# Loading the places of node ranges into VectorE registers: one by one next to their use, in place of ten per group

## The chip, the cores and the metric

The kernel runs on one NeuronCore of a Trainium2 chip. The metric is the device time of one execution in microseconds (us). Before the change it is 1736.52 us, the median of three runs that lie between 1736.14 and 1736.97.

The core has five engines that run side by side, each with its own stream of instructions: TensorE (PE, with its weight loads PEld), VectorE (DVE), ScalarE (ACT), GpSimd (POOL) and SyncE (SP), which here issues transfers. An engine carries out its stream in order. Waits for another engine, address arithmetic in registers and loads into registers stand in that same stream, beside the work on data. In the profile, a `q` behind an engine's name (DVEq) marks what the stream does itself; such instructions are not counted as busy.

## The reference

One layer of a graph network over 12500 nodes with 128 features and 400000 edges, sorted by the node they end at:

```python
Xs = X[src]
m_data = Xs @ W_data.T + b_data
m_ctrl = Xs @ W_control.T + b_control
msg = jnp.where((edge_types == 0)[:, None], m_data, m_ctrl)
agg = jax.ops.segment_sum(msg, dst, num_segments=X.shape[0])
out = agg + (X @ W_self.T + b_self)
x = _layernorm(x + jax.nn.relu(out), axis=-1)
```

The kernel first sums the raw features of the edges by end node and by type, and multiplies the sums by the weights afterwards; this gives the same, since the products are linear.

## The kernel before

The edges are cut into chunks of 128, and 125 chunks form a group; there are 25 groups (`NG`). A group's edges end at some 500 consecutive nodes, for which an accumulator `acc` (128 features by 2 types by 640 nodes) and a count `cnt` are kept in SBUF. Within a group the chunks form windows of two kinds, five of each (`NWIN` is 10):

- `p` windows (five chunks each): GpSimd gathers the 128 feature rows of a chunk from memory (`msg`, L828). The functions are `gathered` and its `chunk`.
- `e` windows (twenty chunks each, five in every fourth group, else four; 107 in all): the rows are picked out of the features held in SBUF by matrix products (L929, `got`), which ScalarE copies to `emsg` (L943). The function is `picked`. For each such window VectorE builds the matrices that sort the edges: `O`, `prod`, `ahead`, `found`, `rank`, `rm`, `rv`, `pick`, for every second window also `om_all`.

In both kinds VectorE builds matrices of zeros and ones from the end nodes (`psel`, `esel`, L533), TensorE multiplies them with the rows into `sums` in PSUM (L755), and VectorE adds the finished `sums` to `acc` and `cnt` (L817). Where in the 640 nodes a window is added depends on the data: that is its place, a whole number. All 250 places (25 groups of 10) are computed on the chip near the start, held to 0 through `R - WMAX` by a max and a min, and stored as `place_i`, one row of 250 numbers on one partition. An add whose address depends on a place needs the place in a register of VectorE; ahead of the add stands a register instruction that works out the address (`ISA` at L817 in the order of instructions, FUSED_REGOPS in the profile).

A `p` window adds to `cnt` and `acc` at one place, an `e` window to `acc` at another. There are 125 `p` windows and 107 `e` windows, so 232 places are used. When the last window of a group has been added, `pass_on` hands the nodes shared with the next group to that group's `acc` and `cnt` (L791, L792).

The order in which each engine gets its instructions is not the program's: a scheduler sorts them by what depends on what and by its own estimate of when things are ready. `tc.issue_after(ins)` asks only that an instruction stand behind `ins` in its engine's stream. Loads of places are queued behind the last add but one that was written ahead of them (`added[-2]`). The main loop runs over the 107 `e` windows and merges into each the chunks of `p` windows, the next windows' matrices, and a group's end (`finish`, L1036 to L1081).

Of the kernel before, what the change touches and what calls it, by code (L numbers as in the profile page):

```python
# [39 lines left out]
WMAX = max(AW, EW)  # L40
CHUNKS = PB + EC
M0 = 50
R = 640
# [17 lines left out]
def kernel(  # L61
# [53 lines left out]
    with ExitStack() as sx:  # L115
        short_path(sx, tc, const, ident, eps, wT, brow, bad, x, src, dst, etype,
                   (w_data, w_ctrl, w_self), (b_data, b_ctrl, b_self), out)
# [89 lines left out]
def short_path(ctx, tc, const, ident, eps, wT, brow, bad, x, src, dst, etype, ws, bs, out):  # L207
    nc = tc.nc
# [32 lines left out]
    raw = {}  # L241
# [500 lines left out]
        return [(0.6, lambda: half(0, NCELL))]  # L742


    acc, added, parts_in, at_places = {}, [], {}, {}

    def sums():
        return ps2.tile([P, 512], FP, name="sums")
# [53 lines left out]
    def place_of(g, i):  # L802

        parts_in[g] = parts_in.get(g, 0) + 1
        if g not in at_places:
            with tc.issue_after(added[-2].ins) if len(added) > 1 else ExitStack():
                _, at_places[g] = nc.values_load_multi_w_load_instructions(
                    raw["place"][0:1, g, :], engines=[nc.vector.engine], min_val=0, max_val=R - WMAX,
                    skip_runtime_bounds_check_because="places are held to this range by a max and a min on the chip",
                )  # L810
        return at_places[g][i]

    def accumulate(at, rows, ps, wide, width):

# [49 lines left out]
    def gathered(g, i):  # L864
# [3 lines left out]
        def add_counts():  # L868
            s["at"] = place_of(g, 2 * i)
            begin_acc(g)  # L870
            rows = cnt[g][:2 * CAP].rearrange("p (o r) -> p o r", o=1)
            accumulate(s["at"], rows, s["ps"][:2 * CAP, 2 * AW:], AW, AW)
# [36 lines left out]
    def picked(w, tiled, ending, before):  # L909
# [83 lines left out]
        def end():  # L993

            early, *more = tiled.get(turns, [lambda: None])
            early()
            gates = add(bounds[turns - 1], NQ)
            for u in more:
                u()
            accumulate(place_of(g, 2 * i + 1), acc_rows(g, 0, 2), s["ps"], EW, EW)  # L1000
            return gates
# [175 lines left out]
    for w in range(pairs):  # L1177
        g, i = each_e[w]
# [182 lines left out]
```

## Time and profile before

| | |
|---|---|
| median of three runs | 1736.52 us |
| the profiled execution | 1736.11 us, of which 1734.3 us is the span from its first to its last instruction |
| granted TensorE clock | 0.992 of full speed |
| PE busy | 1569.6 us, 91% of the span |
| DVE busy | 1550.3 us, 89% |
| POOL busy | 1292.2 us, 75% |
| ACT busy | 1246.5 us, 72% |
| loads of places (L807), in VectorE's stream | 25, from 1064 to 2315 ns each |

The busy share says how long an engine had work, not that it was the one everything waited for. For that the profile has the chain that ended last: it is followed back from the last instruction, at each step to what released that step. A group of instructions is shown with its line, engine, operation, what it writes and reads, its count, its total time and the mean of one, and behind the bar the engine's idle time just ahead of it with what ended that. In a timeline a bracket gives the same for one piece of work.

### The profile page before, as it was taken

What the parts mean: (1) busy time and instruction counts of PE and PEld (TensorE: products, weight loads), DVE (VectorE), ACT (ScalarE), POOL (GpSimd) and SP (SyncE); (2) the same over time, 40 slices, a digit from 0 to 9 for tenths busy, and PEclk for the clock granted to TensorE, in tenths of its full rate; (3) what the DMA queues carried; (4) which work ended last, traced back from release to release, by engine and by line L of the source; (5) the groups of instructions that cost most, each with busy time, mean ns of one, the idle gap of its engine ahead of it and who ended that gap; (6) DMA issues with size and microseconds to landing.
All of it is one profiled execution on the core that took longest, in us unless ns stands there. A gap on an engine that the chain in (4) does not pass through costs nothing.

```text
span 1734.3 us, 67322 instructions
## 1 busy us (share of the span) xinstructions
PE 1569.6 (91%) x28154; PEld 1229.6 (71%) x28154; DVE 1550.3 (89%) x3677; ACT 1246.5 (72%) x2251; POOL 1292.2 (75%) x1061
## 2 busy tenths in 40 slices
PE   0599998999899999999999999999999999999997
PEld 0376777777677777777777777777777777777776
DVE  7898999899798898998998998999998998998983
ACT  5777777677677676777776777776777776777675
POOL 0277888888878788778777787787788787778771
PEclk9999999999999999999999999999999999999999
DMA  7844454444454544454545454445444445444441
GB/s 202 293 130 128 126 154 123 141 151 130 124 157 126 157 136 141 138 157 130 156 131 150 139 150 134 147 117 170 143 148 137 144 137 154 138 145 132 125 126 57
DMA packets 148966, 248.22 MB, mean 143 GB/s; under 512 B 35937, under 2 KB 115260, under 8 KB 148652
## 3 DMA queue, kind: packets, MB, share of 16 engines
q1 hardware_dynamic: 85994, 134.45, 23.4%
q0 software_dynamic: 50032, 102.98, 22.3%
q10 hardware_dynamic: 12626, 6.40, 1.4%
q8 instruction: 222, 3.64, 0.9%
q14 instruction: 92, 0.75, 0.1%
HBM read 226.24 MB, written 17.50 MB: 141 GB/s over the span
## 4 chain that ended last, share of the span: by engine, by line
PE 41%; DVE 39%; ACT 8%; issue 6%; DMA 4%; DVEq 1%; POOL 0%; SPq 0%; ACTq 0%; POOLq 0%
PE sums L755 18%; PE got L929 13%; DVE esel L533 5%; DVE prod L639 4%; ACT emsg L943 4%; PE side L1048 4%; DVE prod L634 3%; DVE pick L741 3%; DVE rv L674 3%; DVE found L641 3%; DVE prod L612 2%; PE side L622 2%; PE side L686 2%; DVE O L533 2%; ACT h L1078 2%
## 5 line engine op out<-in xcount | busy, mean ns | idle before, releaser
L828 POOL DMA_INDIRECT msg<-rows,idx_g x985 | 1222.6, 1241 | 320.4 <-issue 147.2
L943 ACT CAST emsg<-got 128x768 bf16<-128x768 f32 (+1 forms) x1070 | 949.3, 930 | 320.3 <-PE got L929 300.1
L755 PE MATMUL sums<-esel,emsg 128*128 128x176 bf16 x7704 | 693.1, 240 | 3.9 <-DVE acc L817 3.4
L755 PEld LDWEIGHTS <-emsg 128*128 128x128 bf16 x7704 | 566.7, 98 | 117.0 <-issue 108.2
L929 PE MATMUL got<-x,pick 128*32 128x384 bf16 x10486 | 572.9, 330 | 27.7 <-DVE pick L741 13.3
L929 PEld LDWEIGHTS <-pick 128*32 128x32 bf16 x10486 | 242.5, 96 | 155.4 <-issue 24.9
L533 DVE TENSOR_TENSOR esel<-code_col,code 128x1760 bf16<-128x1760 bf16 x321 | 292.1, 910 | 14.5 <-PE sums L755 12.7
L755 PE MATMUL sums<-psel,msg 128*128 128x48 bf16 x2955 | 167.7, 184 | 14.7 <-DVE acc L817 13.0
L755 PEld LDWEIGHTS <-msg 128*128 128x128 bf16 x2955 | 138.8, 97 | 26.8 <-issue 23.7
L639 DVE TENSOR_TENSOR prod<-prod 128x1200 bf16<-128x1200 bf16 x214 | 133.7, 625 | 4.8
L634 DVE TENSOR_TENSOR prod<-O,ahead 128x2000 bf16<-128x2000 bf16 x107 | 128.4, 1200 | 2.5
L533 DVE TENSOR_TENSOR O<-cell_col,blk 128x2000 bf16<-128x2000 bf16 x107 | 127.4, 1191 | 0.9 <-ACT blk L437 0.7
L741 DVE TENSOR_SCALAR pick<-pick,lane_f 128x3200 bf16<-128x3200 bf16 x107 | 113.2, 1058 | 0.8 <-DMA pick<-there 0.8
L817 DVE TENSOR_TENSOR acc<-acc,sums 128x176 f32 (+2 forms) x232 | 66.2, 285 | 52.5 <-PE sums L755 42.2
L904 POOL DMA_INDIRECT both<-rows,idx x54 | 64.2, 1189 | 54.6 <-ACT emsg L943 28.5
L686 PE MATMUL side<-rv,O 128*128 128x64 bf16 x2140 | 83.3, 195 | 21.9 <-DVE rv L674 19.6
L533 DVE TENSOR_TENSOR psel<-near_col,near 128x1200 bf16<-128x1200 bf16 x125 | 95.8, 767 | 0.1
L686 PEld LDWEIGHTS <-O 128*128 128x128 bf16 x2140 | 79.0, 100 | 23.6 <-DVE rv L674 19.8
L674 DVE TENSOR_TENSOR rv<-rm,vals 128x1280 bf16<-128x1280 bf16 x107 | 87.7, 820 | 0.0
L641 DVE TENSOR_REDUCE found<-prod 128x20 f32<-128x600 bf16 x107 | 82.8, 774 | 2.6
L612 DVE TENSOR_TENSOR prod<-O 128x1000 bf16<-128x1000 bf16 x107 | 71.9, 672 | 0.0
L622 PEld LDWEIGHTS <-ltri 128*128 128x128 bf16 x1284 | 41.1, 96 | 38.1 <-issue 36.0
(192 smaller groups left out, 1566.8 us busy)
## 6 DMA issues: line engine op xcount, KB each, us to landing
pick<-there SPq DMA_DIRECT2D x106, 800.0 KB
msg<-rows,idx_g POOLq DMA_INDIRECT x985
acc<-acc_start SPq DMA_DIRECT2D x23, 640.0 KB
rows<-x SPq DMA_DIRECT2D x6, 1344.0 KB
xs<-in_x_dram SPq DMA_DIRECT2D x99, 62.5 KB
out_dram<-h SPq DMA_DIRECT2D x99, 62.5 KB
xt<-in_x_dram ACTq DMA_DIRECT2D x6, 896.0 KB
cnt<-cnt_start SPq DMA_DIRECT2D x22, 160.0 KB
```

Of the source, the lines that this page charges most:

```text
L533: nc.vector.tensor_tensor(sel.rearrange("p n (w t) -> p n w t", t=2), col[:rows].rearrange("p (o w t) -> p o w t", o=1, t=2).to_broadcast( ...
L612: nc.vector.tensor_add(h[:, :2 * CQ], s["O"][:, :2 * CQ], s["O"][:, 2 * CQ:])
L634: nc.vector.tensor_tensor(prod[:, :, :NCELL], s["O"], ahead.rearrange("p (o j) -> p o j", o=1).to_broadcast([P, EC, NCELL]), op=OP.mult,)
L639: nc.vector.tensor_add(prod[:, :, :h], prod[:, :, :h], prod[:, :, h:2 * h])
L641: nc.vector.tensor_reduce(found, prod[:, :, :h], AX.X, OP.add)
L674: placed[:] = [nc.vector.tensor_tensor(rv.rearrange("p c v (r t) -> p c v r t", t=2), rm.rearrange("p c (o r t) -> p c o r t", o=1, t=2).t ...
L686: nc.tensor.matmul(s["rk"][:m, :2 * CAP], s["held"][:, c * NCELL:c * NCELL + m], s["rv"][:, c].rearrange("p v r -> p (v r)"), start=(c == ...
L741: nc.vector.tensor_scalar(t, t, lane_f, None, op0=OP.is_equal)
L755: last = nc.tensor.matmul(out, msg[:, j * D:(j + 1) * D], sel, start=(start and j == 0), stop=stop, skip_group_check=True)
L828: return nc.gpsimd.indirect_dma_start(out=msg, out_offset=None, in_=rows3[:, :], in_offset=bass.IndirectOffsetOnAxis(ap=codes["p", g][0][: ...
L929: last = nc.tensor.matmul(ps[CAP * a:CAP * (a + 1), :], slots[w]["pick"][:, a * NQ + q, :], x3[:, 4 * q + a - a0].rearrange("p j d -> p (j ...
L943: s["out"] = nc.scalar.copy(msg[:, :n], ps[:, :n, :3 * D])
```

## The change

The ten places of a group were loaded by one call into ten registers, when the group's first place was needed, and without a range test. Now each place is loaded by a call of its own into a register, where its window is about to be added, and each load is followed by a test in registers that the value lies between 0 and `R - WMAX`.

```diff
-    acc, added, parts_in, at_places = {}, [], {}, {}
+    acc, added, parts_in = {}, [], {}
...
         parts_in[g] = parts_in.get(g, 0) + 1
-        if g not in at_places:
-            with tc.issue_after(added[-2].ins) if len(added) > 1 else ExitStack():
-                _, at_places[g] = nc.values_load_multi_w_load_instructions(
-                    raw["place"][0:1, g, :], engines=[nc.vector.engine], min_val=0, max_val=R - WMAX,
-                    skip_runtime_bounds_check_because="places are held to this range by a max and a min on the chip",
-                )
-        return at_places[g][i]
+        with tc.issue_after(added[-2].ins) if len(added) > 1 else ExitStack():
+            return nc.vector.value_load(raw["place"][0:1, g, i:i + 1], min_val=0, max_val=R - WMAX)
```

In VectorE's stream there were 25 instructions TENSOR_LOAD for places; there are now 232, and behind each stand two register instructions for its test. Nothing else is added or removed, but the scheduler puts other instructions into another order too. Lines behind the change move up by five: L817 is L812 in the changed kernel, L791 is L786.

The first place is VectorE's stream where group 1 begins, in the kernel before: `esel` and `O` are matrices for `e` windows, the adds to `acc` and `cnt` are those of L817, and L791 and L792 pass group 0's shared nodes on.

```order
L533 TENSOR_TENSOR esel<-code_col,code 128x1760
L533 TENSOR_TENSOR O<-cell_col_143,blk_1333 128x2000
L817 ISA
L817 TENSOR_TENSOR acc<-acc,sums 128x2x88
L807 TENSOR_LOAD place_i
L817 ISA
L817 TENSOR_TENSOR cnt<-cnt,sums 64x120
L817 ISA
L817 TENSOR_TENSOR acc<-acc,sums 128x2x40
L792 TENSOR_TENSOR cnt<-cnt 128x140
L791 TENSOR_TENSOR acc<-acc 128x2x140
```

The same place in VectorE's stream of the changed kernel:

```order
L533 TENSOR_TENSOR esel<-code_col,code 128x1760
L806 TENSOR_LOAD place_i
L806 ISA x2
L806 TENSOR_LOAD place_i
L806 ISA x2
L533 TENSOR_TENSOR O<-cell_col_143,blk_1330 128x2000
L812 ISA
L812 TENSOR_TENSOR acc<-acc,sums 128x2x88
L812 ISA
L812 TENSOR_TENSOR cnt<-cnt,sums 64x120
L812 ISA
L812 TENSOR_TENSOR acc<-acc,sums 128x2x40
```

The load of ten, which stood between two adds, is gone, and two single loads stand behind `esel`, ahead of `O`.

The second place is VectorE's stream a few windows into group 13, in the kernel before: `rs` and `nm` are two short steps of a group's end on 125 rows by 4 numbers, and `parts` and `pk` prepare the next group.

```order
L533 TENSOR_TENSOR esel<-code_col,code 128x1760
L1072 RECIPROCAL rs<-sd 125x4
L511 TENSOR_SCALAR parts<-idx_g 128x125
L1074 SCALAR_TENSOR_TENSOR nm<-mv,rs 125x4
L817 ISA
L817 TENSOR_TENSOR acc<-acc,sums 128x2x88
L512 TENSOR_SCALAR parts<-idx_g 128x125
```

And in the changed kernel:

```order
L533 TENSOR_TENSOR esel<-code_col,code 128x1760
L1067 RECIPROCAL rs<-sd 125x4
L1069 SCALAR_TENSOR_TENSOR nm<-mv,rs 125x4
L806 TENSOR_LOAD place_i
L806 ISA x2
L511 TENSOR_SCALAR parts<-idx_g 128x125
L512 TENSOR_SCALAR parts<-idx_g 128x125
L515 SCALAR_TENSOR_TENSOR pk<-idx_g,vals_23323 128x125
L533 TENSOR_TENSOR psel<-near_col,near_21310 128x1200
L812 ISA
L812 TENSOR_TENSOR acc<-acc,sums 128x2x88
L533 TENSOR_TENSOR esel<-code_col,code 128x1584
```

A single load with its test now stands behind two short instructions, of which the second needs the first, and the add to `acc` comes three instructions later than it did.

The third place is again VectorE's stream in group 0, one window ahead of the first place, where `om_all`, which waits for a small product of TensorE, and `psel` change places. Before:

```order
L817 TENSOR_TENSOR acc<-acc,sums 128x2x40
L533 TENSOR_TENSOR psel<-near_col,near_887 128x1200
L558 TENSOR_SCALAR om_all_193<-slot_col,side 128x7x64 x2
L533 TENSOR_TENSOR O<-cell_col_144,blk_1333 128x2000
L817 ISA
L817 TENSOR_TENSOR acc<-acc,sums 128x2x88
```

In the changed kernel:

```order
L812 TENSOR_TENSOR acc<-acc,sums 128x2x40
L558 TENSOR_SCALAR om_all_193<-slot_col,side 128x7x64 x2
L806 TENSOR_LOAD place_i
L806 ISA x2
L533 TENSOR_TENSOR psel<-near_col,near_887 128x1200
L533 TENSOR_TENSOR O<-cell_col_144,blk_1330 128x2000
L812 ISA
L812 TENSOR_TENSOR acc<-acc,sums 128x2x88
```

`om_all` moves ahead of `psel`, and the load stands right behind it.

## The prediction

> **What bounds the kernel now.** I read the page's head and its shares first, then the chain that ended last, then what VectorE's own stream did around the loads.
>
> ```profile
> span 1734.3 us, 67322 instructions
> PE 1569.6 (91%) x28154; PEld 1229.6 (71%) x28154; DVE 1550.3 (89%) x3677; ACT 1246.5 (72%) x2251; POOL 1292.2 (75%) x1061
> PE 41%; DVE 39%; ACT 8%; issue 6%; DMA 4%; DVEq 1%; POOL 0%; SPq 0%; ACTq 0%; POOLq 0%
> ```
>
> TensorE and VectorE are both busy for nine tenths of the span, and the chain runs through them in equal parts, 41% and 39%. So there is no single bound: the two hand work to each other with little slack. A pause of VectorE is paid where the chain is on VectorE, and is mostly swallowed where it is on TensorE.
>
> The loads of places are not busy time of VectorE, but they hold up its stream. These rows are from the view of one line's instructions (count, then least, median and largest duration), over the whole span and over two short windows:
>
> ```profile
> L807 DVEq TENSOR_LOAD <-place_i x25: 1064/1320/2315, 75.0 to 1660.8; - x25
> ...
> L807 DVEq TENSOR_LOAD <-place_i x1: 2315/2315/2315, 139.8 to 139.8; - x1
> ...
> L807 DVEq TENSOR_LOAD <-place_i x1: 1064/1064/1064, 488.8 to 488.8; - x1
> ```
>
> A load of ten comes in two sizes that alternate from group to group: 12 of the 25 take about 2.3 us, 12 about 1.07 us, and the first 1.32 us; together some 41.7 us. What such a load costs depends on what VectorE still has queued. In the timeline at the first of the two windows it has nothing, in that at the second it has a microsecond of work:
>
> ```profile
> 139.81 0.34 DVE L817 TENSOR_TENSOR acc<-acc,sums 128x176 f32 x1 [0.89 <-PE sums L755]
> ...
> 142.34 0.28 DVE L817 TENSOR_TENSOR cnt<-cnt,sums 64x120 f32 x1 [2.19 <-PE side L622]
> ...
> 142.81 1.31 PE L755 MATMUL sums<-esel,emsg 128*128 128x176 bf16 x15 [1.09 <-DVE acc L817]
> ...
> 489.27 1.05 DVE L741 TENSOR_SCALAR pick<-pick,lane_f 128x3200 bf16<-128x3200 bf16 x1
> 490.23 0.17 DVE L651 MAX8 top<-key 128x8 f32<-128x20 f32 x1
> 490.32 0.25 DVE L817 TENSOR_TENSOR cnt<-cnt,sums 64x120 f32 x1
> ```
>
> At 139.8 the stream had just been let go by TensorE, so the load began together with the add of 0.34 us, VectorE stood idle for 2.19 us, and TensorE then waited 1.09 us for `sums` to be freed. At 488.8 the load ran while VectorE worked off instructions that had been issued ahead; VectorE never stopped. So the stream runs ahead of the work, and only what a load takes beyond that lead is a pause.
>
> The chain in order of time shows what of these pauses was paid:
>
> ```profile
> 140.15 1.99 DVEq L807
> 142.14 0.08 issue
> 142.22 0.07 DVEq L817
> 142.29 0.05 issue
> ...
> 679.63 1.87 DVEq L807
> ...
> 814.85 0.36 DVEq L807
> ...
> 1337.94 0.36 DVEq L807
> ...
> 1599.92 2.17 DVEq L807
> ```
>
> The five pieces are 6.75 us; two more of 0.09 us are on the chain, so it holds 6.9 us of loads. That is what the change can take away for certain.
>
> **The change, part by part.** *Removed:* 25 loads of ten. By the chain the gain is 6.9 us. Its ends: nothing, if TensorE would have held up the same stretches, and 16 us, if none had been covered (41.7 us by VectorE's 39% of the chain). I take 6.9, since it is measured at these very loads.
>
> *Added:* 232 loads of one, each with a test. The trace has one load of a single number on VectorE and one test, both at the end of the kernel, where the flag for the fallback path is read:
>
> ```profile
> L119 SPq TENSOR_LOAD <-bad x1: 480/480/480, 1713.1 to 1713.1; - x1
> ...
> L119 SPq FUSED_REGOPS  x1: 187/187/187, 1713.6 to 1713.6; - x1
> L119 SPq SEQ_ASSERT  x1: 33/33/33, 1713.9 to 1713.9; - x1
> L119 PEldq TENSOR_LOAD <-bad x1: 713/713/713, 1724.0 to 1724.0; - x1
> L119 DVEq TENSOR_LOAD <-bad x1: 309/309/309, 1727.6 to 1727.6; - x1
> ...
> L817 DVEq FUSED_REGOPS  x357: 69/69/69, 76.4 to 1722.5; - x179
> ```
>
> The test is two instructions, 187 and 33 ns on SyncE. On VectorE the load is 0.31 us; the step from a load to the next register instruction is 0.08 us and from there on 0.05 us (the issue rows of the chain above). With the test's first half as on SyncE a place costs 0.31 + 0.08 + 0.19 + 0.05 + 0.03 + 0.05 = 0.71 us of the stream; with that half at the 69 ns that VectorE's address instructions take, 0.59. I take 0.65 us: 151 us of stream in all, against 41.7 before.
>
> What of it becomes a pause depends on what stands ahead. In the order of the changed kernel, 99 of the 232 loads stand right behind an instruction of 0.65 us or more, most often `esel`; those are covered. The other 133 stand behind short ones, 0.28 us in the mean. The mean durations of the commonest are in the groups by shape:
>
> ```profile
> L533 DVE TENSOR_TENSOR esel<-code_col,code 128x1584 bf16<-128x1584 bf16 x107 | 104.2, 974 | 0.0
> ...
> L558 DVE TENSOR_SCALAR om_all<-slot_col,side 128x448 bf16<-128x448 bf16 x107 | 43.0, 439 | 5.3 <-PE side L552 3.7 <-ACT blk L437 0.9 <-ACT emsg L943 0.2
> L630 DVE TENSOR_REDUCE ahead<-side 128x100 bf16<-128x200 f32 x107 | 38.6, 361 | 32.9 <-PE side L622 31.9 <-issue 0.5
> ...
> L647 DVE SCALAR_TENSOR_TENSOR key<-rank,pk 128x20 f32<-128x20 bf16 x107 | 18.5, 173 | 0.0
> ...
> L1074 DVE SCALAR_TENSOR_TENSOR nm<-mv,rs 125x4 f32<-125x4 f32 x24 | 3.8, 157 | 0.2
> ```
>
> If only that one instruction covers (the stream was held until it began, as at 139.8), the pauses are 133 x 0.65 - 36.7 = 50 us, 36.7 being what the short ones take. If the two instructions ahead cover, 48 places are left with 10.7 us. I take the middle, 30 us, since both cases stand in the rows above. Of pauses scattered over VectorE's stream the end pays VectorE's share of the chain: 30 x 0.39 = 11.8 us. The ends are 3.1 us (two instructions cover, 0.59 us a place: 8 us of pauses) and 22.5 us (one covers, 0.71: 58 us).
>
> Behind a load in the stream waits whatever comes next. For 26 of the loads that is the address and the add to `acc` or `cnt`, which frees `sums` for TensorE, and for 13 the pass of `cnt` to the next group; who waits is TensorE, as at 142.81. No transfer is added, and the queues of SyncE and GpSimd hold the same transfers as before. At the end of the kernel the last loads stand ahead of adds that wait for TensorE, and cost nothing unless TensorE is done first.
>
> The Trainium skill's page "DMA: Bandwidth & Descriptors", section "Latency and other measured facts", speaks against the change: it gives a tensor load a floor of about 600 ns and says that the compiler unrolls four times to spread it. The trace has 309 ns on VectorE and 480 on SyncE, both below that floor, so by this case's rows it doesn't hold. With 0.60 in place of 0.31 a place would cost 0.94 us, the pauses would be 34 to 92 us by the two covers, and the sum, as an estimate from that page, 1754 us.
>
> *Moved:* the scheduler, which counts with the loads, puts other work elsewhere. By summing durations along both orders, most instructions keep their place: of the 107 adds that free an `e` window's `sums` some 15 come later and 11 earlier by over 0.2 us, of the adds of `p` windows 12 later and 24 earlier; `om_all` is earlier in 48 of 107 cases. What TensorE waits on these for now:
>
> ```profile
> PE sums L755 <- DVE acc L817: 16.4, 21, 1.8
> PE side L562 <- DVE om_all L558: 14.1, 26, 1.0
> ...
> PE side L504 <- DVE code_r L494: 10.4, 15, 0.9
> ```
>
> These are 41 us, and about a fifth of the places move, so I bound this term by 8 us either way and take nothing, as it goes both ways. The five steps on `bias` near the start move ahead of long work they stood between, and two loads go there; that is at most 2 x 0.65 us, inside the bounds.
>
> *Sum:* -6.9 + 11.8 + 0 = +4.9 us. The profiled execution took 1736.11 us, 0.4 below the median of 1736.52; against the median the forecast is 1741.4 us.
>
> **The rivals.**
>
> *The small pauses are hidden and the large ones go (faster).* Place: the group starts, as at 139.8, 679.6 and 1599.9. If two instructions cover nearly everywhere, the sum is -6.9 + 3.1 = -3.8, so 1732.7; with the order in its favour down to 1725. For it speaks the row at 490.23, where a whole microsecond is hidden, and that at the first place shown above the loads now stand behind `esel`. Against it: 133 loads stand behind short work. It decides when the pauses come to less than 6.9 / 0.39 = 17.7 us, 0.076 us a place.
>
> *It cancels.* The same with pauses between 9 and 27 us: within 0.2% of before, about what a measurement of this kernel can tell from no change (3.5 us), so 1733 to 1740.
>
> *A single load in the stream is dearer than at the end.* TensorE's queue took 713 ns for one number. At that a place costs 1.05 us, the pauses are 46 to 113 us, in the middle 79 x 0.39 = 31 us, and the time is 1761. The loads of ten, at 107 or 230 ns a number, speak against it.
>
> *The change does nothing to VectorE's stream* is excluded by the order: 232 loads stand in it.
>
> **How the numbers follow.** I give the forecast's case, slower by 3.5 to 15 us, 0.40; the dear load or an unlucky order beyond that 0.11; that it cancels 0.19; faster 0.30. So slower 0.51, same 0.19, faster 0.30. The range takes in the full gain with small pauses (-16 + 3.1, 1723.6) and the largest pauses with no gain (+22.5, 1759), and a little of the order's 8 us above: 1723 to 1763. The slower case alone spans 1740 to 1752.
>
> **What the profile of the changed kernel would show.** Right: 232 rows of loads at about 0.31 us each in VectorE's stream, with two register instructions behind; idle of 0.2 to 0.5 us behind short work ahead of many of them; none of 2 us; VectorE's busy time unchanged within 5 us; on the chain, pieces of the loads that add up to more than 6.9 us. Wrong: loads of 0.2 us or less, or DVE's idle time down by more than 10 us with TensorE's too, would make it faster; loads of 0.6 us or more would make it much slower. If the loads' share of the chain is small and the time differs still, it was the order.

## The result and the profile after

The changed kernel takes 1719.82 us (median of six runs, 1711.99 to 1723.35); the kernel before took 1735.88 us beside it (six runs, 1734.46 to 1736.97). The ratio is 0.9904 with a 95% interval of 0.9883 to 0.9924: it is faster by 1%, 16 us. The forecast was 1741.4 us and slower.

The page of the changed kernel, its span, its busy times and its chain by engine:

```profile
span 1718.0 us, 68009 instructions
...
PE 1557.0 (91%) x28154; PEld 1228.9 (72%) x28154; DVE 1556.2 (91%) x3677; ACT 1245.1 (72%) x2251; POOL 1290.1 (75%) x1061
...
DVE 42%; PE 35%; issue 8%; DMA 5%; ACT 4%; DVEq 2%; POOL 1%; ACTq 0%; POOLq 0%; SPq 0%
```

VectorE's busy time rose by 5.9 us, from 1550.3. What fell is the rest of its span: 1734.3 - 1550.3 = 184.0 us before, 1718.0 - 1556.2 = 161.8 us after. So the 16 us come out of the time in which VectorE has no work, although 207 more loads stand in its stream. These are the loads and their tests (count, then least, median and largest ns):

```profile
L806 DVEq TENSOR_LOAD <-place_i x232: 296/304/2044, 44.2 to 1706.0; - x116
L806 DVEq FUSED_REGOPS  x232: 183/190/206, 45.3 to 1706.3; - x116
L806 DVEq SEQ_ASSERT  x232: 23/23/31, 45.5 to 1706.6; - x116
```

They cost the stream what was forecast. The share of VectorE's own queue in the chain went up, from 1% to 2%: the loads and tests hold 26.0 us of the chain in 204 pieces, against 6.9 us for the loads of ten. By themselves they speak for a slower kernel. What fell is shown by VectorE's waits (total us, times, longest us), first before and then after:

```profile
DVE acc L817 <- PE sums L755: 42.2, 35, 7.9
DVE ahead L630 <- PE side L622: 31.9, 50, 2.9
DVE esel L533 <- PE sums L755: 12.7, 15, 1.4
...
DVE cnt L817 <- PE sums L755: 8.3, 9, 2.1
```

```profile
DVE acc L812 <- PE sums L755: 33.2, 32, 6.7
DVE ahead L630 <- PE side L622: 23.3, 44, 1.7
...
DVE esel L533 <- PE sums L755: 9.1, 17, 2.3
...
DVE psel L533 <- issue: 6.3, 16, 0.6
...
DVE cnt L812 <- PE sums L755: 1.3, 4, 0.6
```

The first two waits for TensorE are 17.6 us shorter, and the four rows of before, 95.1 us, are 66.9 us now. New are 6.3 us ahead of `psel` in small pieces. At the place at 139.8 us, where the load of ten had stopped VectorE for 2.19 us, the timeline of the changed kernel has one add behind the other without idle time:

```profile
138.95 0.34 DVE L812 TENSOR_TENSOR acc<-acc,sums 128x176 f32 x1
139.21 0.27 DVE L812 TENSOR_TENSOR cnt<-cnt,sums 64x120 f32 x1
139.40 0.22 DVE L812 TENSOR_TENSOR acc<-acc,sums 128x80 f32 x1
139.55 0.22 DVE L792 TENSOR_TENSOR cnt<-cnt 128x140 bf16<-128x140 bf16 x1
```

TensorE's busy time fell too, from 1569.6 to 1557.0 us, with the same products; that this alone does not shorten the kernel is seen below, where TensorE's order alone brings that busy time to 1562.3 us and the kernel is no faster. The granted clock is not the reason: its mean is 0.994 over the six runs, and 0.993 to 0.994 over the runs of the kernel before beside the first twelve experiments.

Two things had changed at once, the loads and the order in which the scheduler put the rest. The experiments take them apart.

### The profile page after: what moved, and what is told of

Read it like the earlier page. It is cut to its first block, busy times and chain, and to the rows that moved or that the text cites. A ratio compares the mean times of both kernels' runs of the same rounds, so it can differ in the third digit from the quotient of the medians.

```text
span 1718.0 us, 68009 instructions
## 1 busy us (share of the span) xinstructions
PE 1557.0 (91%) x28154; PEld 1228.9 (72%) x28154; DVE 1556.2 (91%) x3677; ACT 1245.1 (72%) x2251; POOL 1290.1 (75%) x1061
## 4 chain that ended last, share of the span: by engine, by line
DVE 42%; PE 35%; issue 8%; DMA 5%; ACT 4%; DVEq 2%; POOL 1%; ACTq 0%; POOLq 0%; SPq 0%
PE sums L755 15%; PE got L924 11%; DVE esel L533 6%; DVE prod L639 4%; DVE prod L634 3%; DVE pick L741 3%; DVE rv L674 3%; PE side L1043 3%; DVE found L641 3%; DMA both<-rows,idx 3%; DVE prod L612 2%; DVE psel L533 2%; ACT emsg L938 2%; DVE O L533 2%; DMA msg<-rows,idx_g 2%
## 5 line engine op out<-in xcount | busy, mean ns | idle before, releaser
L533 DVE TENSOR_TENSOR esel<-code_col,code 128x1760 bf16<-128x1760 bf16 x321 | 292.6, 912 | 11.8 <-PE sums L755 9.1
L812 DVE TENSOR_TENSOR acc<-acc,sums 128x176 f32 (+2 forms) x232 | 66.6, 287 | 34.1 <-PE sums L755 33.2
(192 smaller groups left out, 1562.3 us busy)
```

The costliest lines, as they stand in the source:

```text
L533: nc.vector.tensor_tensor(sel.rearrange("p n (w t) -> p n w t", t=2), col[:rows].rearrange("p (o w t) -> p o w t", o=1, t=2).to_broadcast( ...
```

## The experiments

Several kernels below have an engine's order prescribed. The same function does it in all: each instruction is made to be issued behind the one ahead of it in a list, without a semaphore; loads and tests of places are left out of the lists. Between two loads or orders everything else stays as it was.

```diff
+def in_given_order(tc):
...
+    for engine, text in _ORDER.items():
...
+        for a, b in zip(order, order[1:]):
+            tc.add_manual_dep(
+                mine[b], mine[a].name,
+                mybir.DependencyInfo(mybir.DependencyClass.NoSync, mybir.DependencyReason.DATA), reason="given order",
+            )
```

### Loads of ten in the changed kernel's order, single loads in the order of before

The kernel before, with the lists of all five engines taken from the changed kernel:

```diff
+_ORDER = {
+    'EngineType.Pool':
...
+    'EngineType.PE':
...
+        in_given_order(tc)
```

> Loads of ten as before the change, but every other instruction on every engine in the changed kernel's order. If the gain of 16 us came from the other order, this takes about 1720 us plus what the loads of ten cost against single ones, so 1715 to 1728. If it came from the loads themselves (no stops of 2.3 us at the starts of odd groups), this takes about 1736, 1732 to 1740.

The reverse is the same edit to the changed kernel, with the lists taken from before:

```diff
+        in_given_order(tc)
```

> Single loads with their tests as after the change, but every other instruction on every engine in the order of the kernel before. If the order gave the gain, this takes 1736 to 1741 us (the prediction's sum without a change of order). If the loads gave it, about 1720, 1715 to 1725.

Loads of ten in the new order: 1721.13 us, ratio 0.9915 (0.9895 to 0.9935). Single loads in the old order: 1742.62 us, ratio 1.0043 (1.0027 to 1.0058), where before took 1734.41 us. The order is worth the whole gain and the single loads, in the old order, cost 8 us, a little more than either expectation had. From the page and the waits of single loads in the old order:

```profile
span 1740.4 us, 67993 instructions
...
DVE 42%; PE 40%; issue 7%; ACT 6%; DMA 3%; DVEq 2%; SPq 0%; POOL 0%; ACTq 0%; POOLq 0%
```

```profile
DVE ahead L663 <- PE side L655: 28.6, 47, 1.4
DVE esel L566 <- PE sums L788: 18.1, 20, 2.4
...
DVE psel L566 <- issue: 11.6, 14, 3.3
```

Here too VectorE stands ahead of `psel`, 11.6 us that the profile puts down to "issue"; in 8.7 of them a load stands directly ahead in the stream. `esel` waits longer than before (18.1 us for 12.7). The adds' wait for `sums` is 12.5 us shorter than with loads of ten in the same order (29.7 for 42.2): a part of the pauses takes the place of waits. The two effects don't add up in full. In the new order loads of ten and single loads take the same time within their intervals; in the old one they differ by 8 us. Why the cost of the single loads is not seen in the new order stays open.

### Loads of ten, with rows that start at other addresses

The loads of ten had come in two sizes that alternate by group. A row of ten numbers is 40 bytes, so every other row starts 8 bytes off a multiple of 16. Two kernels in the order of before space the rows by 48 bytes; in one they start at a multiple of 16:

```diff
-        place_i = raw["place"] = keep.tile([1, NG, NWIN], I32, name="place_i")
+        wide = keep.tile([1, NG, 12], I32, name="place_i")
+        place_i = raw["place"] = wide[:, :, 0:0+NWIN]
```

> The kernel before, with the row of ten places stored 48 bytes apart in place of 40, so that each row starts at a multiple of 16 bytes; the order stays the same. If the size of a load of ten goes by where its row starts, all 25 take about 1.07 us. Then the loads' theory says 12 x 1.23 = 15 us less stop on VectorE, so 1722 to 1730; the order's theory says at most the share of it that was on the chain, 1732 to 1736.

and in the other 8 bytes behind it:

```diff
-        place_i = raw["place"] = keep.tile([1, NG, NWIN], I32, name="place_i")
+        wide = keep.tile([1, NG, 12], I32, name="place_i")
+        place_i = raw["place"] = wide[:, :, 2:2+NWIN]
```

> The same with each row starting 8 bytes behind a multiple of 16. If the start decides, all 25 loads take about 2.3 us, 13 x 1.23 = 16 us more stop on VectorE than before. The loads' theory: 1745 to 1753. The order's theory: 1736 to 1741.

The loads in the first and in the second:

```profile
L808 DVEq TENSOR_LOAD <-place_i x25: 1061/1066/1319, 76.9 to 1655.9; - x25
```

```profile
L808 DVEq TENSOR_LOAD <-place_i x25: 2279/2285/2527, 76.3 to 1667.3; - x25
```

Where the row starts makes the size: 1.07 or 2.28 us for the same ten numbers. The times are 1730.65 us (0.997, 0.9957 to 0.9983) and 1742.62 us (1.0044, 1.0029 to 1.006). Each lies between its two expected ranges, so neither theory had the size right. Between the two kernels the loads differ by 25 x (2.285 - 1.066) = 30.5 us of the stream and the times by 12.0 us, which is 39%; the intervals of the two ratios leave room for about 31 to 53%. That this is VectorE's share of the chain in the profile before doesn't confirm the prediction's rule, which took that share of the pauses and not of the loads' whole time. VectorE's idle time directly behind loads is 6.8 us in the first kernel and 15.4 us in the second, but 15.4 us in the kernel before as well, which takes 8 us less than the second. Where the second pays these 8 us isn't shown.

### Single loads without the test

The changed kernel without the range tests of the 232 places:

```diff
-            return nc.vector.value_load(raw["place"][0:1, g, i:i + 1], min_val=0, max_val=R - WMAX)
+            return nc.values_load(
+                raw["place"][0:1, g, i:i + 1], engines=[nc.vector.engine], min_val=0, max_val=R - WMAX,
...
+            )
```

> The changed kernel without the tests behind its loads; all other instructions keep the changed kernel's order. A place then takes 0.3 us of VectorE's stream in place of 0.6. If the pauses behind loads are paid by VectorE's share of the chain, 5 to 9 us less than the changed kernel, so 1711 to 1715. If they are mostly swallowed, 1717 to 1720.

1716.54 us, ratio 0.9903 (0.9886 to 0.992), where before took 1732.95: the same ratio as with the tests. In the new order 232 times 0.2 us of the stream are worth nothing that can be measured; the two intervals leave room for some 5 us.

### TensorE's order: more and fewer changes of size

In the new order TensorE changes less often between products with 32 and with 128 weight columns (1326 times for 1388), so this was a candidate. One kernel takes the changed kernel's order with 248 such changes more, by splitting 124 runs of products; the other takes the order of before with 84 fewer, by joining 46. Both differ from the given order in TensorE's list alone:

```diff
+    'EngineType.PE':
...
+        in_given_order(tc)
```

> The changed kernel with one product of sums put ahead of the last four row-picking products at 124 places of TensorE's order, so that TensorE changes between products with 32 and with 128 weight columns 248 times more often (1574 times, 1326 in the changed kernel, 1388 before); hardly anything else moves. If these changes, about 0.1 us each in the trace, are paid, and are part of the 16 us: 12 to 25 us more than the changed kernel, so 1732 to 1745. If the order's gain is about waits alone: 1718 to 1726.

> The kernel before, loads of ten, but at 46 places of TensorE's order a few small products that stood inside a run of row picking stand behind it, so that TensorE changes between 32 and 128 weight columns 1304 times in place of 1388. If the changes are paid: 4 to 8 us less, 1726 to 1731. If what waits for the moved products matters more: 1734 to 1745.

With the splits it takes 1713.34 us, ratio 0.9891 (0.9876 to 0.9907): no slower than the changed kernel. With the joins it takes 1732.17 us, ratio 1.0002 (0.9991 to 1.0013). TensorE's busy time does move, from 1557.0 to 1580.9 us with 248 changes more and from 1569.6 to 1561.0 us with 84 fewer, about 0.1 us a change both times. The Trainium skill's page "TensorEngine Tiling (Array Packing)", section "Key Properties", says that changing the tiling mode drains TensorE. The rise of the busy time agrees with that; no time of these two runs speaks for a price that the end pays here.

### One engine's order at a time

Loads of ten, with the changed kernel's order prescribed to TensorE alone, all others left to the scheduler:

```diff
+_ORDER = {
+    'EngineType.PE':
...
+}
...
+        in_given_order(tc)
```

> The kernel before, loads of ten, with TensorE's instructions alone in the changed kernel's order; the scheduler orders the other engines by itself, and VectorE's order then stands between the two kernels' orders. If TensorE's order is what gave the gain: 1717 to 1726, with TensorE busy about 1557 us. If it was VectorE's order: 1731 to 1737.

And to VectorE alone:

```diff
+_ORDER = {
+    'EngineType.DVE':
...
+}
...
+        in_given_order(tc)
```

> Loads of ten, and VectorE's own instructions alone forced into the changed kernel's order; TensorE, ScalarE, GpSimd and the queues are left to the scheduler. If VectorE's order carries the gain: 1717 to 1724 us, VectorE's idle time near 155 us as in the changed kernel. If the orders of several engines must fit together: 1730 to 1738 us, idle near 175 us as with TensorE's order alone.

TensorE's order: 1736.99 us, ratio 1.0027 (1.0014 to 1.004). VectorE's order: 1711.94 us, ratio 0.9872 (0.9857 to 0.9887), below the changed kernel's own 0.9904 and below the expected range. From the page and the waits with TensorE's order, then the same with VectorE's:

```profile
span 1736.9 us, 67341 instructions
...
PE 1562.3 (90%) x28154; PEld 1231.9 (71%) x28154; DVE 1554.7 (90%) x3677; ACT 1245.0 (72%) x2251; POOL 1287.3 (74%) x1061
```

```profile
DVE acc L846 <- PE sums L784: 43.6, 47, 3.2
DVE ahead L659 <- PE side L651: 32.1, 55, 1.6
```

```profile
span 1711.8 us, 67316 instructions
...
PE 1568.0 (92%) x28154; PEld 1224.9 (72%) x28154; DVE 1550.0 (91%) x3677; ACT 1247.2 (73%) x2251; POOL 1278.5 (75%) x1061
```

```profile
DVE ahead L659 <- PE side L651: 28.5, 45, 1.4
DVE acc L846 <- PE sums L784: 23.8, 26, 3.4
```

With VectorE's order the wait of the adds for `sums` is nearly halved (42.2 to 23.8 us), VectorE's busy time is that of before (1550.0 us), and its span without work is 161.8 us for 184.0: that is nearly the whole of the 22.5 us between the spans. So the changed kernel's order of VectorE is enough for the gain, and that of TensorE is not. It is not VectorE's order by itself, since the scheduler ordered the other engines anew: TensorE's stream there differs from that of before in 138 stretches and from that of the changed kernel in 130. (With TensorE's order prescribed, VectorE's differs from that of before in 119.) VectorE's new order with all others left as before was not run.

A part of the 22 us goes with the clock. The four runs with VectorE's order all have a granted clock of 0.998, where the kernel before had 0.994 in the mean of its 15 runs. Those 15 runs are longer by about 1 us for each 0.001 of clock less, so the estimate from them is 4 us, which is most of the way by which this kernel lies below the changed one. Whether the order raised the clock isn't shown. It is still the best of all these kernels, and it has loads of ten.

Against before, the changed kernel's list for VectorE differs in 254 short stretches of 2 to 22 instructions, 1237 of 3677 instructions in all.

### Other orders from the same scheduler

Three kernels change only behind which earlier add a load is queued, and leave the order to the scheduler. Loads of ten, issued earlier:

```diff
-            with tc.issue_after(added[-2].ins) if len(added) > 1 else ExitStack():
+            with tc.issue_after(added[-6].ins) if len(added) > 5 else ExitStack():
```

> Loads of ten, held back only to the sixth last addition instead of the second last, and the scheduler free: another order drawn by the same scheduler, with the same loads. If orders differ by chance by about 1 per cent: anywhere from 1715 to 1745 us. If loads of ten as such lead the scheduler to the slower order: 1730 to 1738 us.

The same edit to the changed kernel, so single loads issued earlier:

```diff
-        with tc.issue_after(added[-2].ins) if len(added) > 1 else ExitStack():
+        with tc.issue_after(added[-6].ins) if len(added) > 5 else ExitStack():
```

> Single loads with tests, held back only to the sixth last addition, scheduler free. If single loads as such lead the scheduler to a good order: 1715 to 1723 us. If it was one lucky order: anywhere from 1715 to 1750 us. Apart from the order, each single load may go further ahead of its use, which by the loads' own cost changes the time by under 3 us.

And single loads issued later:

```diff
-        with tc.issue_after(added[-2].ins) if len(added) > 1 else ExitStack():
+        with tc.issue_after(added[-1].ins) if added else ExitStack():
```

> Single loads with tests, each held back to the last addition, scheduler free. Single loads good as such: 1715 to 1725 us. One lucky order: anywhere from 1715 to 1750 us.

Loads of ten early: 1726.90 us, ratio 0.9963 (0.995 to 0.9977). Single early: 1723.10 us, 0.9937 (0.9923 to 0.995). Single late: 1731.04 us, 0.9985 (0.9976 to 0.9994). So with before (1) and after (0.9904) five orders that the scheduler made by itself spread over 1%, with loads of ten in two of them and single loads in three. None of the other four was slower than before; that single loads lead to better orders as such isn't shown by three against two. Nor does likeness to the good order make a good one: the last kernel's order of VectorE differs from the changed kernel's in 139 stretches with 536 instructions (that of before in 254 with 1237), and it gains 0.15% where the changed kernel gains 1%.

### One gather's place on GpSimd

The longest stop of VectorE amid the kernel before is 7.92 us. Its timeline shows the cause far from VectorE:

```profile
457.20 0.94 POOL L904 DMA_INDIRECT both<-rows,idx  x1 [0.30 <-issue]
...
460.19 0.51 ACT L991 COPY last<-both 64x384 bf16<-64x384 bf16 x1 [6.28 <-DMA both<-rows,idx]
460.60 0.20 ACT L694 CAST cell<-side 128x64 bf16<-128x64 f32 x1
...
460.86 0.21 PE L707 MATMUL side<-ident_b,cell 128*32 128x25 bf16 x4 [5.68 <-ACT cell L694]
...
463.86 0.34 DVE L817 TENSOR_TENSOR acc<-acc,sums 128x176 f32 x1 [7.92 <-PE sums L755]
```

GpSimd issued a gather late, ScalarE stood 6.28 us for it with the copy `cell` queued behind, TensorE waited for `cell`, and VectorE for TensorE. Issuing these gathers four others earlier, in the order of before for all engines, was to show what such stops are worth; of the lists only GpSimd's differs from before:

```diff
+    'EngineType.Pool':
...
+        in_given_order(tc)
```

> Every engine in the order of before, loads of ten; on GpSimd alone each gather into both is issued four gathers of messages (about 5 us) earlier. ScalarE's copy of both then should wait for it far less than 21.4 us. If that wait carries VectorE's long stops (the 7.9 us one at 464 us, 4.4 at 333, 5.1 at 1079): 1718 to 1728 us. If it is hidden or other waits take its place: 1731 to 1737 us.

It came out at 2267.37 us, ratio 1.1186 (1.1159 to 1.1213), on a chip on which before took 2027.26 us. Both expectations failed. GpSimd's own rows show what happened:

```profile
L937 POOL DMA_INDIRECT both<-rows,idx x54: 912/1245/4506, 74.5 to 2236.5; - x54
its engine sat idle before it (us, times) until:
  ACT emsg L976: 233.5, 33
  ACT idx L612: 145.4, 17
...
who waited for it (us, times):
  ACT last L1024: 4.8, 1
```

GpSimd now stands for `emsg` and `idx`, 379 us together, with the gathers of messages queued behind. On the same chip, in the kernel of the "other 173" stretches below, these two rows are 64.7 us. The granted clock is lower too (0.892); how much of the loss goes with it isn't shown. What the stops are worth could not be seen there at all: ScalarE's wait for these gathers, 21.4 us in the kernel before, is not among the waits of that other kernel on this chip, so there was nothing to take away. That such stops are not what made the difference between the two kernels is seen without it: ScalarE's wait for this gather is 21.4 us in the kernel before and 26.8 us in the changed one:

```profile
ACT last L986 <- DMA both<-rows,idx: 26.8, 14, 5.2
```

### Parts of VectorE's order

To find which of the 254 stretches matter, three kernels with loads of ten prescribe VectorE's list alone: the changed kernel's order in some stretches and that of before in the rest. They differ in the one list:

```diff
+    'EngineType.DVE':
...
+        in_given_order(tc)
```

The 81 stretches in which an add changes sides with another instruction:

> Loads of ten; VectorE's order is that of before except in the 81 short stretches in which the changed kernel has an addition (of sums into acc or cnt) on another side of some other instruction; there it is the changed kernel's. TensorE and the other engines are left to the scheduler. If VectorE's additions stood too early and their being moved is the gain: 1710 to 1720 us, idle ahead of the additions of 176 down from 52 to about 35 us. If it is the sum of many small moves of all kinds: 1722 to 1730 us.

The other 173:

> The other 173 short stretches: VectorE's order is the changed kernel's there and that of before in the 81 with additions. If the additions carry the gain: 1730 to 1737 us. If many small moves share it: 1718 to 1728 us.

The 122 stretches of the first half:

> VectorE's order is the changed kernel's up to group 10 (850 us into the span, 122 of the 254 stretches in which they differ) and that of before afterwards. In the trace with the changed kernel's whole order 17 us of 22 us had been gained by group 10. If stretches act where they stand: 1714 to 1720 us. If a gain is given back later: above 1725 us.

And the first of these again, beside the best order with the aligned rows of 48 bytes:

> The kernel of the 81 stretches with additions once more, since the chip of its first run took 2027 us for the kernel before. If VectorE's additions stood too early and their being moved is the gain: a ratio of 0.985 to 0.991 (1708 to 1718 us where before takes 1733). If many small moves of all kinds share the gain: 0.993 to 0.998. If none of it lies in these stretches: 0.999 to 1.003.

> Loads of ten whose rows start at multiples of 48 bytes, with VectorE's order of the changed kernel. If the shorter loads' gain (0.3 per cent) adds to that of the order (1.28 per cent): a ratio of 0.983 to 0.986. If the time of the loads is hidden in this order: 0.986 to 0.989.

These runs were on chips on which before took 2027.26 and 2022.73 us. The ratios there: adds 1.0018 (0.9999 to 1.0036), rest 1.0037 (1.0013 to 1.0061), first half 0.9959 (0.994 to 0.9978); then adds 1.0026 (1.001 to 1.0043), and the best order with aligned rows 1.0005 (0.9985 to 1.0025). The last combines two changes that had given 1.28% and 0.3% on the other chips, and here gives nothing; its clock, 0.965 in the mean for 0.971 of before, accounts for some 6 us, as an estimate by the 0.9 us for each 0.001 of clock that the runs of before show there. The page and TensorE's groups of the second run with the adds' stretches show another kernel, as it were:

```profile
PE 1694.0 (84%) x28154; PEld 1271.5 (63%) x28154; DVE 1567.8 (77%) x3677; ACT 1257.0 (62%) x2251; POOL 1249.6 (62%) x1061
...
PE 64%; DVE 12%; ACT 12%; issue 8%; another core or an unknown queue 2%; DMA 2%; DVEq 0%; SPq 0%; ACTq 0%; POOL 0%
```

```profile
L958 PE MATMUL got<-x,pick 128*32 128x384 bf16 x10486 | 637.8, 337 | 125.3 <-ACT emsg L972 58.6 <-issue 27.9 <-ACT last L974 14.0
```

The kernel before, on its own chip, has this row for the same products:

```profile
L929 PE MATMUL got<-x,pick 128*32 128x384 bf16 x10486 | 572.9, 330 | 27.7 <-DVE pick L741 13.3 <-ACT emsg L943 12.7 <-ACT cell L694 0.3
```

There TensorE holds 64% of the chain and VectorE 12%, so VectorE's order should have little to decide. Which of its moves carry the gain on the other chips therefore stays open: the adds, the rest and the first half were not measured there.

## Why the prediction was wrong

*Removed.* Taken as 6.9 us from the chain, with an upper end of 16 us. No run measures it by itself. The pair of kernels with other row starts shows 39% of a difference of 1.2 us a load being paid; if the rest were paid at that share, the 41.7 us of before would be worth 16 us, the upper end. The load at 488.8, hidden whole, speaks against that.

*Added.* Right in the price of a place (0.30 + 0.19 + 0.02 us and the steps between them, 0.62 in the median, taken as 0.65), about right in the pauses (forecast 30 us; VectorE's idle time directly behind single loads in the old order is 31.9 us, some of it with a wait for TensorE), and right in that the end pays for some of it. The net of removed and added was forecast as +4.9 us, and measured alone, in the old order, it is 0.0043 x 1734 = 7.5 us (4.7 to 10.1). So the sum of these two terms was right in sign and within its interval, though neither term was measured alone: if the loads of ten were worth 6.9 us, the single ones cost 14.4, for 11.8 forecast; if 16, then 23.5, above the forecast's upper end, and the net came close by luck.

*Moved.* This is the step that failed: "I bound this term by 8 us either way and take nothing, as it goes both ways." It is 24 us with single loads (from ratio 1.0043 to 0.9904 with only the order exchanged) and 15 us with loads of ten (to 0.9915); with VectorE's order alone prescribed and the others drawn anew it is 22 us, of which about 4 go with the clock. The bound was drawn from TensorE's waits for VectorE, 41 us in three rows, of which a fifth seemed to move. It was VectorE's waits for TensorE that fell: adds, `ahead`, `esel` and `cnt` had 95.1 us in the four rows of before shown above, and none was among those on which the term was bounded. The adds were counted as moving both ways, 15 later and 11 earlier, and so as cancelling. An explanation, argued and not shown, is that the two don't cancel: an add that comes after `sums` is ready has nothing to wait for, and one that comes too early stops VectorE. Which of the moved instructions carry the gain stays open.

*The rivals.* The time lies 5 us below that of the first (1732.7 to 1725), and not by its mechanism: the small pauses are not hidden in the old order. The dear single load is refuted, 304 ns against the 713 of TensorE's queue. So is, with it, the sum of 1754 us from the Trainium skill's page "DMA: Bandwidth & Descriptors", section "Latency and other measured facts": its floor of some 600 ns for a tensor load is twice what VectorE's loads took.

*What the profile was to show.* Right: 232 loads at 0.31 us with two register instructions each, more than 6.9 us of them on the chain. Nearly right: VectorE's busy time within 5 us (5.9), no stop of 2 us for a load (one load took 2.04 us). Of the signs of being wrong, VectorE's idle time fell by over 10 us, but TensorE's hardly (164.7 to 161.0 us of the span).

The range, 1723 to 1763 us, missed 1719.82 because the term for the order was 8 us where 24 would have been needed, and because even the 8 us, said to go both ways, were put in, and only in part, above alone. Taken off the lower end of 1723.6 as well they would have reached 1715.6 and held the time, but by luck, since that end stood for a gain from the loads that they did not give.

## What to carry to other kernels

Where two engines share the chain and a scheduler sets the order, an edit that makes it sort anew has two effects, and the second can be larger than the first: here 8 us for the loads and 15 to 24 us for the order. Take them apart before believing in either, by prescribing one kernel's order to the other, and engine by engine; and give the order's term the spread that other orders of the same scheduler show, here 1%. Before keeping a gain of this kind, look at which engine holds the chain on the chip at hand, since the same order, with aligned rows, gave nothing where TensorE held 64% of it.

## What the runs showed of the hardware

A load of ten numbers into VectorE's registers takes 1.07 us from a row that starts at a multiple of 16 bytes, counted from the start of the tile, and 2.28 us from one that starts 8 bytes behind it: 107 or 228 ns a number, against 304 ns for one alone. Other starts were not measured for loads of ten.

The same kernel took 1733 to 1736 us on some chips and 2023 to 2027 us on two others, which were used only for the last six experiments, so chip and time of the run are not parted. The kernel before was not traced there; the trace of the one with the adds' stretches, set against that of before on its own chip, shows nearly the same busy time of VectorE (1567.8 us for 1550.3), 8% more of TensorE (1694.0 us for 1569.6), and twice the idle time of TensorE (332.2 us of the span for 164.7). Ahead of `got` this is 125.3 us for 27.7, in the rows above: 58.6 us wait for ScalarE's copies, and 27.9 us by "issue" are stops for which the profile shows no wait. The granted clock is lower, 0.970 for 0.992. By the 0.9 us for each 0.001 of clock that the runs of before show there, that is some 20 us of the 290, as an estimate; what else slows TensorE there wasn't found.
